# Row-by-row tiles at both ends of a four-layer graph network, with a layer's shifts made once and elu added a quarter at a time

## The chip, the cores and the metric

The kernel runs on one core of a Trainium2 chip, in one launch. The metric is the device time of the whole launch in microseconds (us), the median of several executions. One further execution was taken with the hardware profiler. Its instructions belong to TensorE (PE, whose weight loads are listed apart as PEld), VectorE (DVE), ScalarE (ACT), GpSimd (POOL) and SyncE (SP, which here only issues DMA transfers).

## What is computed

The input x holds 8 graphs (batches) of 2048 nodes with 128 features, and one 0/1 adjacency matrix of 2048 x 2048 serves all of them. Four layers follow one another; each adds to x a function of the normalized, rectified x. Layers 0 and 3 are graph attention with one head, layer 1 is attention with four heads under the same mask, layer 2 is a masked mean. What matters here are layers 0 and 3:

```python
e = leaky_relu(s1[:, :, None] + s2[:, None, :])          # slope 0.2
e = where(adj[None, :, :] > 0, e, very_negative)
h_prime = einsum('bij,bjo->bio', softmax(e, -1), h)      # layer 0: + h, then elu
```

s1 and s2 are two numbers per node, made from h. Each output row i needs a softmax over the 2048 nodes j, hence a maximum over the allowed j, the exponentials, their sum, and a product with h.

## The kernel before, in words

The 2048 nodes of a batch are 16 row tiles of 128. Four row tiles are a quarter (512 rows, one buffer of x). Layers 0 and 3 use six groups of row tiles, `GROUPS`: four of three tiles and two of two.

**A graph attention layer by groups** (`gat_loop`, L450) keeps the scores transposed: j is on the partitions and the rows i of a group lie along the free dimension, so the exponentials can go into TensorE as weights without a transpose. For this, two things must lie along the free dimension of every partition: s1 of the group's rows, and the shift m of each row (the leaky value of its maximum). The order of a group is:

- `gat_maximum` (L440 to L447): for each row tile, one DVE instruction of 128 x 2048 on a broadcast copy of s2 (`s2b`) and a mask (`pmg`, fetched from DRAM) gives the largest allowed s2 of each row, `mn`.
- `shifts` (L475 to L483): three DVE instructions of a few columns turn s1 and `mn` into `cab`.
- `spread` (L485), through `along_free` (L400 to L411): DVE transposes `cab` (L404), four transfers write the rows to DRAM (`rowd`, L407), and one reads them back to all 128 partitions (`ab`, L410).
- Eight steps `jp`, each for two j tiles: `leaky` (L510, two ACT instructions), `lowered` (L516, DVE), `exps` (L520, ACT), `masked` (L525, DVE), `product` (L536, 2 x 3 or 2 x 2 matmuls into `gacc`). The stages of successive steps overlap, each stage one step later than the one before it.
- `ended` and `closed` (L551 on): reciprocals, and the layer's own `finish`. In layer 0, `finish` makes `hq` on DVE (L663) and `ex` on ACT (L667), and adds elu to x with two DVE instructions for each row tile (L672, L673). In layer 3 it adds to x (L892), and when the row tile is the last of its quarter it stores the quarter.

`ahead(k)` prepares group k during the first five steps of group k - 1.

**The order of the work.** The order on PE, DVE, ACT and POOL is written out by hand; each engine works through its list in order. SP's order is set by a planner. There are three parts:

- The **head** (batch 0): the masks are made from the adjacency matrix, layer 0 of batch 0 runs by groups (with the maxima of a group inside the loop, and one empty step after each group), and a quarter goes on to the projections of layer 1 (`before_attention`) as soon as its row tiles are done.
- The **middle**: layer 1 of all batches, as `mains`, 256 blocks of 12 short steps. Between these steps stand the other layers of the neighbouring batches: layer 2, then layer 0 of the next batch, then layer 3 of the last one. `work` spreads a list of steps by weight; `locked` puts three steps of `mains` to each step of a `gat_loop`. In layer 0 of batches 1 to 7 all 16 maxima are made ahead, beside the aggregation of layer 2 (`merged(agg, top)`); in layer 3 they are made in the loop.
- The **tail**: layers 2 and 3 of batch 7, with nothing of layer 1 beside them.

Of the kernel before, what the change touches and what calls it, by code (L numbers as in the profile page):

```python
# [18 lines left out]
P = 128  # L19
# [12 lines left out]
def gnn_kernel(  # L32
# [201 lines left out]
    ones = const.tile([P, P], F32, name="ones")  # L234
# [5 lines left out]
    w0T = const.tile([P, P], F32, name="w0T")  # L240
# [159 lines left out]
    def along_free(col, dst, n):  # L400


        row = small("row", (P, 32))
        nc.vector.transpose(row, col)  # L404
        d = new(dr2, "rowd", "rowd", (T, P))
        for g in range(4):
            nc.sync.dma_start(  # L407
                out=d[0:n, g * 32 : (g + 1) * 32], in_=row[g * 32 : g * 32 + n, :]
            )
        nc.sync.dma_start(  # L410
            out=dst, in_=d[0:n, :].rearrange("t p -> (t p)").partition_broadcast(P)  # L411
        )
# [22 lines left out]
    def gat_rows(st):  # L435

        st["s2b"] = new(sp2, "s2b", "s2b", (P, N))
        along_free(st["s2n"], st["s2b"], T)
# [12 lines left out]
    def gat_loop(st, finish, maxima, gap):  # L451
# [23 lines left out]
        def shifts(k):  # L475
            i0, n = GROUPS[k]
            s1 = st["s1"][:, i0 : i0 + n]
            u = small("gu", (P, 3))[:, 0:n]
            nc.vector.tensor_tensor(u, s1, st["mn"][:, i0 : i0 + n], ALU.subtract)
            cab = next_of("cab", cabs)  # L480
            nc.vector.tensor_copy(cab[:, 0:n], s1)
            nc.vector.scalar_tensor_tensor(cab[:, n : 2 * n], u, ALPHA, u, ALU.mult, ALU.max)
            gr[k]["cab"] = cab  # L483

        def spread(k):  # L485
            n = GROUPS[k][1]
            t = new(abp, "ab", "ab", (P, 2 * n * P))
            along_free(gr[k]["cab"], t, 2 * n)
            gr[k]["s1"], gr[k]["m"] = t[:, 0 : n * P], t[:, n * P : 2 * n * P]

        def ahead(k):
            if k >= len(GROUPS):
                return []
# [65 lines left out]
        for fns in ahead(0):  # L559
            steps.add(2.0, *fns)  # L560

        items = []
        for k in range(len(GROUPS)):
            items += [(k, jp) for jp in range(T // 2)] + [None] * gap
# [3 lines left out]
        for step in range(len(items) + len(stages) - 1):  # L568
            fns = []
            if step < len(items) and items[step]:  # L570
                k, jp = items[step]
                if jp == 0:
                    nxt = ahead(k + 1)
                if 0 < jp <= len(nxt):
                    fns += nxt[jp - 1]
            for s in reversed(range(len(stages))):
                if 0 <= step - s < len(items) and items[step - s]:
                    fns.append(at(names[s], lambda f=stages[s], a=items[step - s]: f(*a)))
            steps.add(2.6, *fns)
# [75 lines left out]
    def layer0_loop(b, st, maxima=False, gap=1):  # L655
# [3 lines left out]
        def finish(i0, n, acc, rec):  # L659
            hq = new(hpp, "hp", "hp", (P, 3, P))  # L660
            ex = new(hpp, "ex", "ex", (P, 3, P))
# [7 lines left out]
            def add():  # L669
                for q in range(n):  # L670
                    xg = xb[(i0 + q) // 4][:, (i0 + q) % 4, :]
# [5 lines left out]
        return gat_loop(st, finish, maxima, gap)  # L677
# [174 lines left out]
    def layer3(b, gap=1, maxima=True):  # L852
# [35 lines left out]
        def finish(i0, n, acc, rec):  # L888
            for q in range(n):
# [5 lines left out]
                if it % 4 == 3:  # L895
                    g = it // 4
# [5 lines left out]

        tops = [at("maxi", lambda it=it: gat_maximum(st, it)) for it in range(T)]
        return pre, gat_loop(st, finish, maxima, gap), tops


# [354 lines left out]
    with tc.manual_schedule(engines=ENGINES):  # L1261
# [16 lines left out]
        loop = layer0_loop(0, st0, True)  # L1278
        quarters, queue, others = before_attention(0), [], masks_all[n:]
        start = len(loop) - 9 * len(GROUPS) - 6  # L1280
        for _ in range(3):
            run([others.pop(0)])
        n_late = len(others)
        for k, step in enumerate(loop):
# [3 lines left out]
            for g, group in enumerate((1, 2, 3, 5)):  # L1288
                if k == start + 9 * group + 13:
                    queue.extend(quarters([g]))  # L1290
            if queue:
                run([queue.pop(0)])
        run(others + queue)
# [76 lines left out]
        for b in range(B):  # L1370
            side = Steps()
            if b >= 1:
                pre2, agg = layer2(b - 1)
                side.extend(pre2)
                pre3, loop3, _ = layer3(b - 1, 0)
# [5 lines left out]
            if b + 1 < B:  # L1381
# [3 lines left out]
                side.extend(merged(agg, top) if agg else top)  # L1385
                loop0 = layer0_loop(b + 1, sts[b + 1], gap=0)

                side[-8:-8] = loop0[:5]
# [31 lines left out]
        pre3, loop3, _ = layer3(B - 1)  # L1420
# [60 lines left out]
```

## Time and profile before

| | |
|---|---|
| median of 3 runs | 4548.66 us (4547.90 to 4550.93) |
| the profiled execution | 4556.48 us, of which the span of its instructions is 4554.6 us |
| mean granted clock of TensorE | 0.956 of full speed |
| head: first matmul of layer 1 starts | 253.6 us |
| tail: layer 3's broadcast s2 (`s2b`) is used first | 4423.8 us |
| last store issued | 4551.3 us |

Times within the profile are microseconds from the span's start. A group row of the profile gives the line and engine, the operation, output and inputs by name, the shapes, how many there were, the busy time and the mean duration, and then the idle time of the engine just before them and what ended it. A matmul on 32-bit numbers has two records in the trace: the program has 4096 matmuls into `gacc`, the trace 8192. Where the text speaks of a pace, it is the distance from start to start; it is shorter than the duration, since an engine begins the next instruction before the last one is finished.

A table by stretches of time gives, for each stretch, its length, the busy time and number of instructions of each engine, the clock granted to TensorE as a share of full speed, the share of the DMA engines' time and their GB/s.

### The profile page before, as it was taken

The page shows a single profiled execution, that of the slowest core. Times are in us where ns is not written, and L with a number is a line of the kernel's source. Part 1 is how long each engine was busy: PE and PEld are TensorE (multiplying, and loading weights), DVE is VectorE, ACT ScalarE, POOL GpSimd, SP SyncE. Part 2 cuts the span into 40 slices and gives each one's busy share as a digit, 9 for nine tenths or more (in the row PEclk, how much of TensorE's full clock was granted, in tenths as well). Part 3 has the DMA queues.
Part 4 walks back from the last instruction along what each step waited for, and adds up shares of the span by engine and source line. Part 5 has one row for each costly group of instructions (what it writes and reads, how often), then busy time and mean ns, then how long its engine had stood idle before and what let it go on. Part 6 is the DMA issues. An engine that isn't in the chain of part 4 may idle for free.

```text
span 4554.6 us, 87375 instructions
## 1 busy us (share of the span) xinstructions
PE 4009.2 (88%) x33290; PEld 2809.7 (62%) x33290; DVE 3796.6 (83%) x7529; ACT 3613.6 (79%) x5121; POOL 553.7 (12%) x549
## 2 busy tenths in 40 slices
PE   3679998998999989998899988999899989998966
PEld 2545765666657666576666756566665766655636
DVE  5968877889889898888988889799888898748939
ACT  6658985898859888698868988598895989858916
POOL 1220011004100130002300031001300010000000
PEclk6889999999999999999999999999999999999978
DMA  8522133223241323313242232412333223222232
GB/s 305 153 69 59 54 92 110 66 71 106 82 140 53 94 83 107 109 60 105 77 128 75 67 101 84 144 49 72 102 103 116 59 69 113 58 75 71 64 100 75
DMA packets 312192, 423.32 MB, mean 93 GB/s; under 512 B 65318, under 2 KB 181724, under 8 KB 307676
## 3 DMA queue, kind: packets, MB, share of 16 engines
q1 hardware_dynamic: 311264, 417.51, 30.2%
q8 instruction: 263, 4.31, 0.4%
q14 instruction: 157, 1.29, 0.1%
q10 hardware_dynamic: 508, 0.22, 0.0%
HBM read 365.78 MB, written 55.98 MB: 93 GB/s over the span
## 4 chain that ended last, share of the span: by engine, by line
PE 31%; DVE 25%; ACT 22%; issue 5%; DMA 2%; SPq 0%; DVEq 0%; POOL 0%; ACTq 0%
PE pagg L798 7%; DVE e L963 7%; ACT e L970 6%; PE pt L982 6%; ACT eT L987 6%; PE gacc L536 6%; DVE dump L447 5%; PE sc L946 5%; ACT ge L510 5%; DVE ge L516 4%; DVE ge L525 3%; PE acc L997 3%; ACT ge L520 3%; DVE ln_s L341 1%; PE ph L397 1%
## 5 line engine op out<-in xcount | busy, mean ns | idle before, releaser
L987 ACT COPY eT<-pt 128x1024 f32<-128x1024 f32 x1024 | 996.2, 1017 | 440.8 <-PE pt L982 439.5
L536 PE MATMUL gacc<-haug,ge 128*128 128x129 f32 x8192 | 1106.6, 285 | 156.4 <-DVE ge L525 121.5
L982 PE MATMUL pt<-ident,e 128*128 128x128 f32 x8192 | 1043.7, 279 | 168.6 <-DVE amh L963 126.1
L536 PEld LDWEIGHTS gacc<-haug,ge 128*128 128x128 f32 x8192 | 1008.2, 197 | 297.7 <-issue 215.3
L982 PEld LDWEIGHTS pt<-ident,e 128*128 128x128 f32 x8192 | 928.2, 144 | 268.5 <-DVE amh L963 149.8
L970 ACT ACTIVATE e<-e,amn 128x2048 f32<-128x2048 f32 x512 | 1035.1, 2022 | 12.7 <-DVE amn L963 12.7
L510 ACT ACTIVATE ge<-ab,s 128x384 f32<-128x384 f32 (+1 forms) x1536 | 808.0, 583 | 107.7 <-DMA ab<-rowd 89.2
L963 DVE CUSTOM_DVE_ANT_0 e<-sc,pm 128x1024 f32<-128x1024 f32 x512 | 625.0, 1221 | 265.6 <-PE sc L946 220.6
L946 PE MATMUL sc<-ks,qr 32*128 32x512 f32 x4096 | 746.6, 658 | 59.5 <-ACT eT L987 41.5
L963 DVE CUSTOM_DVE_ANT_0 e<-sc,pm,amh 128x1024 f32<-128x1024 f32 x512 | 657.5, 1284 | 76.0 <-PE sc L946 3.6
L520 ACT ACTIVATE ge<-ge 128x768 f32<-128x768 f32 (+1 forms) x768 | 601.3, 784 | 134.0 <-DVE ge L516 133.1
L525 DVE SCALAR_TENSOR_TENSOR ge<-mg,ge 128x768 f32<-128x768 fp8e4 (+1 forms) x768 | 666.3, 868 | 24.4 <-ACT ge L520 23.9
L516 DVE TENSOR_TENSOR ge<-ge,ab 128x768 f32<-128x768 f32 (+1 forms) x768 | 665.7, 867 | 16.3 <-ACT ge L510 13.1
L447 DVE CUSTOM_DVE_ANT_0 dump<-s2b,pmg 128x2048 bf16<-128x2048 f32 x256 | 588.9, 2300 | 36.9 <-DMA pmg<-pm_all 18.3
L997 PE MATMUL acc<-eT,vv 128*32 128x256 f32 x8192 | 562.9, 393 | 1.9 <-ACT eT L987 1.9
L997 PEld LDWEIGHTS acc<-eT,vv 128*32 128x32 f32 x8192 | 216.3, 110 | 496.4 <-issue 407.7
L349 POOL TENSOR_SCALAR ln_r<-ln_mv 128x4 f32<-128x4 f32 x128 | 86.4, 675 | 3528.2 <-DVE ln_mv L343 3280.7
L946 PEld LDWEIGHTS sc<-ks,qr 32*128 32x128 f32 x4096 | 235.3, 187 | 222.4 <-ACT eT L987 112.6
L798 PE MATMUL pagg<-mt,hm 128*128 128x512 fp8e4 x1536 | 353.6, 380 | 11.7 <-DVE agT L816 11.7
L798 PEld LDWEIGHTS <-hm 128*128 128x128 bf16 x1536 | 148.0, 98 | 185.5 <-issue 31.4
L350 POOL TENSOR_TENSOR ln_r<-ln_r,neg_half 128x4 f32<-128x4 f32 x128 | 161.4, 1261 | 10.7
L383 PE MATMUL ptr<-ident,h 128*128 128x128 f32 x512 | 88.2, 297 | 41.1 <-DVE h L357 12.6
(131 smaller groups left out, 2591.3 us busy)
## 6 DMA issues: line engine op xcount, KB each, us to landing
pmg<-pm_all SPq DMA_DIRECT2D x256, 256.0 KB
mg<-mg_all SPq DMA_DIRECT2D x128, 384.0 KB
pm<-pm_all SPq DMA_DIRECT2D x128, 256.0 KB
qr<-qd SPq DMA_DIRECT2D x1024, 32.0 KB
mt<-mt_all SPq DMA_DIRECT2D x64, 512.0 KB
ab<-rowd SPq DMA_DIRECT2D x64, 384.0 KB
adj<-in_adj_dram SPq DMA_DIRECT2D x16, 1024.0 KB
s2b<-rowd SPq DMA_DIRECT2D x16, 1024.0 KB
```

Of the source, the lines that this page charges most:

```text
L447: nc.vector.tensor_tensor_reduce(dump, st["s2b"], pm, UP, HIGHEST, ALU.add, ALU.min, st["mn"][:, it : it + 1])
L510: nc.scalar.activation(e[:, c, :], gr[k]["s1"], AF.Prelu, bias=st["s2"][:, j : j + 1], alpha=ALPHA)
L516: nc.vector.tensor_tensor(e, e, bc_mid(gr[k]["m"], 2), ALU.subtract)
L525: nc.vector.scalar_tensor_tensor(e, mt, BIG, e, ALU.mult, ALU.min)
L536: nc.tensor.matmul(gr[k]["acc"][:, q, :], e[:, c, q * P : (q + 1) * P], st["haug"][:, j, :], start=(j == 0 and q == 0), stop=(j == T - 1), ...
L798: nc.tensor.matmul(st["pa"], st["hm"][:, j, s, :], st["mt", g, j // 8][:, j % 8, :], start=(j == 0 and s == 0), stop=(j == T - 1 and s == ...
L946: nc.tensor.matmul(blk["sc"][g // 2][:, (g % 2) * 512 : (g % 2 + 1) * 512], blk["q"][r, t * P : (t + 1) * P], ks_t[b, hh][r, :], start=Tru ...
L963: nc.vector.tensor_tensor_reduce(e[:, c], blk["sc"][h], pm[:, c], UP, least, ALU.add, ALU.min, to)
L970: nc.scalar.activation(blk["e"][t], blk["e"][t], AF.Exp, scale=-1.0, bias=blk["mn"][:, t : t + 1], accum_out=blk["ao"]["sum"][:, t, blk["h ...
L982: nc.tensor.transpose(pt[:, c, t, :], blk["e"][t][:, j * P : (j + 1) * P], ident)
L987: nc.scalar.copy(eT, blk.pop(("pt", w)).rearrange("p c t n -> p c (t n)"))
L997: nc.tensor.matmul(pair["acc"][g * HD : (g + 1) * HD, blk["hh"] % 2, :], vv_t[blk["b"], blk["hh"]][:, j, :], blk["eT"][w][:, g, :], start= ...
```

## The change

There are three parts.

**Row by row.** In the head's layer 0 and in the tail's layer 3 only the first three groups (row tiles 0 to 8) are worked by groups, and without the empty steps. The other seven row tiles (9 to 15) are worked row by row by the new `gat_rowwise`: i stays on the partitions and all 2048 j lie along the free dimension, so no `shifts`, no `spread` and no `gat_maximum` is needed; instead the exponentials must be transposed by TensorE and copied back. The two lists of steps are merged by weight, and the row-by-row list ends at 0.9 (head) or 0.85 (tail) of the other.

**Shifts once.** `along_free` is split into `to_rows` (transpose and four writes) and `from_rows` (the broadcast read). Where the maxima are made ahead, which is in layer 0 of batches 1 to 7, the shifts of all 16 row tiles are made once, with the first group, and each group reads its part with two transfers of half the size. Since these shifts need all 16 maxima, the maxima now end at 0.9 of the aggregation, and the first five steps of the loop are put three steps before the aggregation's end, where they stood eight before.

**elu by quarters.** `finish` of layer 0 adds elu with two DVE instructions for all row tiles of a group that lie in one quarter, where it had two for each row tile. A quarter goes on when its last row tile is done, in any order.

Two buffers of the start (`ones`, `w0T`) move into a rotating pool.

```diff
+    def to_rows(col, n):
         row = small("row", (P, 32))
         nc.vector.transpose(row, col)
-        d = new(dr2, "rowd", "rowd", (T, P))
+        d = new(dr2, "rowd" if n <= T else "rowa", "rowd", (T if n <= T else 2 * T, P))
         for g in range(4):
             nc.sync.dma_start(
                 out=d[0:n, g * 32 : (g + 1) * 32], in_=row[g * 32 : g * 32 + n, :]
             )
+        return d
+
+    def from_rows(d, i, n, dst):
         nc.sync.dma_start(
-            out=dst, in_=d[0:n, :].rearrange("t p -> (t p)").partition_broadcast(P)
+            out=dst, in_=d[i : i + n, :].rearrange("t p -> (t p)").partition_broadcast(P)
         )
...
+        def shifts(k):
+            i0, n = GROUPS[k]
+            if maxima:
+                gr[k]["cab"] = shifts_of(i0, n)
+            elif k == 0:
+                st["rowa"] = to_rows(shifts_of(0, T), 2 * T)
 
         def spread(k):
...
+            if maxima:
+                from_rows(to_rows(gr[k]["cab"], 2 * n), 0, 2 * n, t)
+            else:
+                for c in range(2):
+                    from_rows(st["rowa"], c * T + i0, n, t[:, c * n * P : (c + 1) * n * P])
...
+    def gat_rowwise(st, finish, its):
...
+        def leaky(it):
...
+            e[it] = new(ep, "e", "er", (P, N))
+            nc.scalar.activation(
+                e[it], st["s2b"], AF.Prelu, scale=ALPHA, bias=st["s1n"][:, it : it + 1],
+                alpha=1.0 / ALPHA,
+            )
+
+        def lowest(it):
+            pm = new(mg, "pm", "pmg", (P, N), I8)
+            nc.sync.dma_start(out=pm, in_=pm_all[it])
+            mn[it] = small("rmn", (P, 1))
+            nc.vector.tensor_tensor_reduce(
+                e[it], e[it], pm, UP, HIGHEST, ALU.add, ALU.min, mn[it]
+            )
+
+        def exps(it):
+            sm_[it] = small("rsum", (P, 1))
+            nc.scalar.activation(
+                e[it], e[it], AF.Exp, scale=-1.0, bias=mn.pop(it), accum_out=sm_[it]
+            )
+
+        def turned(it, h):
+            pt = psum("ptg", (P, 8, P))
+            for c in range(8):
+                j = 8 * h + c
+                nc.tensor.transpose(pt[:, c, :], e[it][:, j * P : (j + 1) * P], ident)
+
+            def read():
+                eT[it, h] = new(tp, "eT", "eTg", (P, 8, P))
+                nc.scalar.copy(eT[it, h], pt)
+
+            later(read)
+
+        def product(it, h):
+            if h == 0:
+                acc[it] = new(psa, "acc", "racc", (P, 1, P))
+            t = eT.pop((it, h))
+            for c in range(8):
+                j = 8 * h + c
+                nc.tensor.matmul(
+                    acc[it][:, 0, :], t[:, c, :], st["haug"][:, j, 0:P],
+                    start=(j == 0), stop=(j == T - 1),
+                )
+
+        def ended(it):
+            rec = small("rrec", (P, 1))
+            nc.vector.reciprocal(rec, sm_.pop(it))
+            close[it] = finish(it, 1, acc.pop(it), rec)
...
+        stages = [
+            (7, closed), (6, ended), (0, leaky), (1, lowest), (2, exps),
+            (3, lambda i: turned(i, 0)), (4, lambda i: turned(i, 1)),
+            (4, lambda i: product(i, 0)), (5, lambda i: product(i, 1)),
+        ]
...
             def add():
-                for q in range(n):
-                    xg = xb[(i0 + q) // 4][:, (i0 + q) % 4, :]
+                ended.update(range(i0, i0 + n))
+
+                for g in range(i0 // 4, (i0 + n - 1) // 4 + 1):
+                    lo, hi = max(i0, 4 * g), min(i0 + n, 4 * g + 4)
+                    xg = xb[g][:, lo - 4 * g : hi - 4 * g, :]
+                    q = slice(lo - i0, hi - i0)
                     nc.vector.scalar_tensor_tensor(xg, ex[:, q, :], 1.0, xg, ALU.min, ALU.add)
                     nc.vector.scalar_tensor_tensor(xg, hq[:, q, :], 0.0, xg, ALU.max, ALU.add)
...
-        loop = layer0_loop(0, st0, True)
+        loop = layer0_loop(0, st0, True, 0, [0, 1, 2], 0.9)
...
-                side.extend(merged(agg, top) if agg else top)
+                side.extend(merged(agg, top, 0.9) if agg else top)
                 loop0 = layer0_loop(b + 1, sts[b + 1], gap=0)
 
-                side[-8:-8] = loop0[:5]
+                n = len(side) - 3 * bool(agg)
+                side[n:n] = loop0[:5]
...
-        pre3, loop3, _ = layer3(B - 1)
+        pre3, loop3 = layer3(B - 1, 0, True, [0, 1, 2], 0.85)
```

In the numbers of the stages, a row tile starts every second step and its stage s runs s steps after its start.

## The prediction

> **What bounds the kernel now.** I read the page first, then the tables by stretches of time for the head, one layer 0 of the middle and the tail, then the groups and the order of time in the tail. The page says that nothing idles much on average, which hides that the stages differ:
>
> ```profile
> PE 4009.2 (88%) x33290; PEld 2809.7 (62%) x33290; DVE 3796.6 (83%) x7529; ACT 3613.6 (79%) x5121; POOL 553.7 (12%) x549
> ```
>
> The tables by stages tell them apart. Tail, then head, then a layer 0 of the middle:
>
> ```profile
> 4453.00:4463.00 10.00, 7.93 (x67) 7.43 (x66) 10.00 (x11) 7.29 (x14) 0.00 (x0) 1.00 0.45 129
> 4463.00:4473.00 10.00, 4.09 (x20) 4.12 (x21) 9.96 (x19) 5.54 (x10) 0.00 (x0) 0.66 0.25 70
> 4473.00:4483.00 10.00, 8.27 (x68) 7.69 (x68) 10.00 (x12) 7.71 (x14) 0.00 (x0) 1.00 0.26 84
> sum 132.00, PE 73.62 PEld 70.42 DVE 118.70 ACT 80.78 POOL 0.00; mean PE 5.66 PEld 5.42 DVE 9.13 ACT 6.21 POOL 0.00
> ```
> ```profile
> 130.00:155.00 25.00, 15.05 (x98) 14.10 (x96) 24.02 (x37) 15.01 (x25) 0.00 (x0) 0.80 0.80 191
> 180.00:205.00 25.00, 17.46 (x120) 15.12 (x119) 24.86 (x47) 17.56 (x31) 10.73 (x4) 0.93 0.42 122
> ```
> ```profile
> 1420.00:1440.00 20.00, 19.53 (x186) 14.47 (x181) 18.20 (x35) 20.00 (x31) 0.00 (x0) 1.00 0.12 32
> 1480.00:1500.00 20.00, 19.27 (x186) 14.10 (x185) 17.40 (x36) 20.00 (x33) 0.00 (x0) 1.00 0.22 77
> ```
>
> In both ends DVE is the bound (third engine column: full), with PE and ACT far below. In the middle's layer 0 ACT is full, PE nearly, and DVE has some 10% to spare. So DVE work is worth its time at the ends and little in the middle.
>
> **The ends, row by row.** First what a row tile costs by groups. In the tail's order of time L516 and L525 of three-tile groups start 0.87 us apart (4451.50, 4452.37, 4453.23), so a step jp takes 1.74 us of DVE; for two-tile groups 1.20 (a start each 0.60, head). Eight steps per group, plus a maximum (2.21 + 0.08):
>
> ```profile
> L510 ACT ACTIVATE ge<-ab,s 128x384 f32<-128x384 f32 x64 | 35.1, 601 | 23.2 <-DMA ab<-rowd 23.1
> L516 DVE TENSOR_TENSOR ge<-ge,ab 128x768 f32<-128x768 f32 x32 | 30.5, 953 | 5.7 <-ACT ge L510 5.7
> L525 DVE SCALAR_TENSOR_TENSOR ge<-mg,ge 128x768 f32<-128x768 fp8e4 x32 | 30.3, 947 | 0.0
> L447 DVE CUSTOM_DVE_ANT_0 dump<-s2b,pmg 128x2048 bf16<-128x2048 f32 x13 | 29.7, 2284 | 0.0
> L520 ACT ACTIVATE ge<-ge 128x768 f32<-128x768 f32 x32 | 26.9, 840 | 23.6 <-DVE ge L516 23.0
> ```
>
> (Groups of the tail; "x" is the count, then busy time and mean ns.) DVE of a loop before: 32 x 1.74 + 16 x 1.20 + 16 x 2.29 + 16 x 0.27 (L892) + small ones of 3 = 120; the trace has 118.7. After: 24 x 1.74 = 41.8, nine maxima 20.6, seven `lowest`, the closing 4.3 + 3. `lowest` is not in the trace; it is L447 with a 32-bit output. Below stands L447 (2.29), above the pair L963 of twice 1024 (1.22 + 1.28 = 2.50). I take 2.3, its nearest row: 16. **Sum 86, 34 less.**
>
> ACT before: 32 x 1.83 (starts of L520 in the tail: 4449.78, 4451.61) + 16 x 1.42 (two-tile) = 81; trace 80.8. After: 24 x 1.83 = 43.9 and, for each of seven rows, `leaky` of 2048 (L510 takes 493 ns for 256 and 601 for 384 elements, so 0.86 ns each, 2.03 us), `exps` (L970 of the same form, starts 1.98 apart) and two copies like L987 (0.92 apart): 5.85 x 7 = 41. **Sum 85, 4 more.** The slope could be off for `leaky`: between 1.6 (0.65 ns, the copy's 1024 in 0.92 doubled) and 2.2, so 3 less or 1 more.
>
> PE keeps its 256 products (two records each) and gains 112 transposes. Warm pace: 0.237 us for a product (12 weight loads of 6 products in 1.41), 0.216 for a transpose (L982, 16 loads of 8 in 1.73): 60.7 + 24.2 = 85. At the tail's present clock: 73.6 + 24.2/0.83 = 103. **PE becomes the bound, 85 to 103**, with DVE and ACT close behind.
>
> Here the clock decides. It was 1.00 from 4453 to 4463 and 0.66 from 4463 to 4473, where DVE did maxima and PE waited 6.5 us; in the middle, with PE over 90% busy, it is 1.00. Transposes fill these gaps, so I take 0.93: 91 us. The Trainium skill ("TensorE: Matmul & The Clock Gate", Part 1) says that a window of about 3.4 us without work halves the clock, which the row above agrees with; its Part 4 says that transpose-mode work does not count as busy, which speaks against this change. If that held, 112 transposes would leave the clock at today's, and the sum would be the 103 above. The middle, with L982 at its warm pace and 1.00, speaks for the other.
>
> Path in the tail. `s2b` is used at 4423.8. The first two masks are loaded; the third instruction on DVE is now row 9's `lowest`, whose mask needs the first buffer (free at 4426.1, landing 2.8 later as now), and the group's third maximum follows: `shifts` end near 4434.2 instead of 4431.7, `ab` lands near 4441 instead of 4438.6. In this time row 9 and 10 do `leaky`, `lowest` and `exps`, so PE starts near 4436 instead of 4447. Then 91 of PE, 4 for the time to 4441 when only a row's transposes are there, 4 for five last steps at ACT's 1.83 and the drain, and 4 which I choose for in-order engines that wait for each other with all three at 85: 4539 instead of 4551. **Tail 12 less** (bounds: 85 with nothing lost, 4525: 26 less; 103 and 10 lost, 4557: 6 more). At the very end one three-tile group closes two quarters, 0.3 of L892 and a second store (0.4 to issue): 0.7, inside these bounds.
>
> Head. DVE falls by the same 34, and by 1.3 for elu. But `shifts` of the first group come later: behind `lowest` of row 9 (2.3), its wait for a mask (about 3), and the degrees with 16 instructions L1234 (4.3, now ahead of it, as the masks' last steps fall into the first tenth of a shorter loop). `ab` lands near 120 instead of 109.4. From there PE has 256 x 0.25 + 112 x 0.22 + 9 for two quarters = 98, less 4 already done; the loop ends near 222 with 8 lost, instead of 242. Then two quarters (tiles 4 to 7 and 8 to 11 both wait for the last group) go on instead of one: 243.2 to 253.6 now, and 4 more for the second, whose instructions follow the first's on each engine, and 2.5 for a three-tile drain. 239 instead of 253.6. **Head 13 less** (bounds as in the tail: 24 less to 8 more).
>
> **The middle.** Per layer 0 of batches 1 to 7, shifts once take 5 x (0.16 x 3 + 0.20) = 3.4 us off DVE and 20 small writes off SP, and elu 32 x 0.29 = 9.2 becomes 16 instructions at 0.29, 0.42 or 0.56 (start overhead 0.16 and 0.133 per 128, from L672 and L829's 0.69 for 512) = 6.8. Together 5.8 us. It is beside ACT: in 1360 to 1540 ACT idles 3.3 of 180, so at most that much can come back; if ACT's cover were gone all 5.8 would count.
>
> Against it stands a wait that is moved. At the start of each layer 0 ACT waits for `ab`:
>
> ```profile
> 1344.29 0.21 DVE L404 STREAM_TRANSPOSE row<-cab 128x32 f32<-128x32 f32 x1
> 1353.47 1.12 ACT L510 ACTIVATE ge<-ab,s 128x384 f32<-128x384 f32 x2 [5.61 <-DMA ab<-rowd]
> ```
>
> The chain from the transpose through DRAM takes 9.2 us, of which 5.6 are waited, with layer 1's copies L987 and exponentials L970 queued behind. In the new order the same two copies and one exponential stand between transpose and `leaky`, and no maximum is left on DVE behind them. The first half of `ab` (192 KB) lands earlier than 384 KB did: the 4.9 us from issue to use may lose 1 or nothing; the wider writes (32 rows for 6) may add 1. Bounds: 2 less to 3.6 more (all 9.2 open). I take 0, and 1 us back from ACT's idle time: 7 x 1 = **7 less** (bounds 7 x 5 less, 7 x 3.6 = 25 more). Later groups read rows long written; `ab` waits there are few already.
>
> **Sum:** 12 + 13 + 7 = 32; the span 4554.6 becomes 4522.6, its execution 4524.5. That execution stood 7.8 above the median, so the median becomes 4548.7 - 32 = **4517**.
>
> **Rivals.**
> 1. *All three engines overlap well* and the clock is full: tail 20, head 20, middle 15: 4494. For it: each row stage has a step of slack. Against: in-order queues at equal load.
> 2. *They hold each other up*: PE waits for `exps`, ACT's copy for the transposes, DVE for `leaky`; a fifth of the time is lost: tail 4, head 5, middle 4: 4536.
> 3. *The middle gives the ends back*: `ab` at the start of seven layers is waited for with all 9.2 us: 25 more against 25 less: 4549. For it: the spread stands three steps ahead of the aggregation's end, not eight. Against: the order above.
> 4. *Slower: the clock stays low.* If PE stays near 0.66 in both ends, 85 becomes 129: tail ends 44 later than the 85 would, at 4436 + 129 + 12 = 4577 (26 more), head 20 more, middle 7 less: 4588. It decides where PE's work fills the present loop: 4551 - 4436 - 12 = 103, a mean clock of 85/103 = 0.83. For it: today's tail has just this mean. Against: the gaps that lower it are filled.
> 5. *It doesn't do what it says*: "once a layer" holds for seven layers only, since the middle's layer 3 makes its maxima in the loop; this is already in the sum.
>
> **Chances.** Forecast 45% (4502 to 4530), rival 1 17%, rival 2 20%, rival 3 9%, rival 4 9%. The measurement tells 0.2%, about 9 us, from no change. Faster: forecast, 1 and most of 2, 79%; same: part of 2 and 3, 10%; slower: 4 and part of 3, 11%. The range goes from rival 1 to just short of rival 3's time: 4492 to 4545.
>
> **What would show it.** In the tail: DVE busy near 86 and PE over 85 of the loop, clock above 0.9, 4539 or so for the last addition. PE under 80% busy beside a clock under 0.8 would show rival 4; all three engines near 80% busy, rival 2. `leaky` of a row at 2.0 us and `lowest` at 2.3. In the head: `ab` first used near 120, the first matmul of layer 1 near 239. In the middle: the wait for `ab` at the start of layer 0 still 5 to 6 us, ACT full after it. I am wrong if a wait for a mask (`pmg`, two buffers, now shared by maxima and rows) is large on DVE, or the middle's period of batches changes by over 3 us.

## The result, and the profile after

The changed kernel took **4542.0 us** (median of 10 runs, 4531.4 to 4545.3) beside 4550.6 for the kernel before on the same chip: a ratio of **0.9973** with a 95% interval of 0.9964 to 0.9982. That is 8.5 us faster, where 32 were forecast. The profiled execution took 4542.2 us with a span of 4540.4.

The span divides at the first and the last matmul `sc` of layer 1 into head, middle and tail:

| us | before | after | difference | forecast |
|---|---|---|---|---|
| head, to the first `sc` | 253.6 | 237.3 | -16.3 | -13 |
| middle | 4059.0 | 4084.1 | **+25.1** | -7 |
| tail, from the last `sc` | 242.0 | 218.9 | -23.1 | -12 |
| span | 4554.6 | 4540.4 | -14.2 | -32 |

(The profiled execution before lay 6 us above its median, the one after on it; so 14 in the spans are 8.5 in the medians.) Both ends gained more than forecast, and the middle lost most of it.

The page of the changed kernel, busy time of each engine:

```profile
PE 4028.9 (89%) x33514; PEld 2828.8 (62%) x33514; DVE 3703.9 (82%) x7159; ACT 3618.5 (80%) x5051; POOL 533.2 (12%) x549
```

DVE lost 93 us and ACT gained 5. As before, this average says nothing of where the time went. The table by stretches of the tail does (length, then PE, PEld, DVE, ACT, POOL with their counts, clock, DMA share, GB/s); the last line sums 4428 to 4540:

```profile
4448.00:4458.00 10.00, 5.13 (x23) 4.84 (x24) 6.25 (x6) 8.31 (x10) 0.00 (x0) 0.50 0.26 72
4458.00:4468.00 10.00, 8.75 (x64) 8.55 (x64) 8.38 (x14) 10.00 (x14) 0.00 (x0) 0.84 0.20 54
4468.00:4478.00 10.00, 8.91 (x80) 8.70 (x79) 8.62 (x11) 10.00 (x13) 0.00 (x0) 1.00 0.35 105
4488.00:4498.00 10.00, 9.05 (x66) 8.93 (x67) 9.85 (x19) 6.82 (x11) 0.00 (x0) 0.83 0.26 82
4508.00:4518.00 10.00, 9.57 (x86) 9.37 (x85) 6.90 (x9) 10.00 (x17) 0.00 (x0) 1.00 0.01 2
sum 112.00, PE 78.75 PEld 76.51 DVE 86.21 ACT 82.63 POOL 0.00; mean PE 7.16 PEld 6.96 DVE 7.84 ACT 7.51 POOL 0.00
```

DVE, which was full in such stretches before, now has 1.4 to 3.1 of 10 us to spare in three of these, where ACT is full and PE close behind; from 4488 to 4498 DVE still leads (9.85) and ACT has 6.82. Over the whole 112 us no engine works more than 86. The head and a layer 0 of the middle, in the same columns:

```profile
130.00:155.00 25.00, 21.69 (x164) 20.92 (x164) 22.61 (x32) 25.00 (x34) 0.00 (x0) 0.87 0.77 205
180.00:205.00 25.00, 22.14 (x192) 21.57 (x193) 19.11 (x33) 23.95 (x36) 0.00 (x0) 1.00 0.18 57
1420.00:1440.00 20.00, 19.53 (x184) 14.08 (x179) 17.93 (x32) 20.00 (x30) 0.00 (x0) 1.00 0.24 51
1480.00:1500.00 20.00, 19.28 (x187) 14.10 (x185) 17.13 (x33) 20.00 (x32) 0.00 (x0) 1.00 0.26 90
```

Well inside a layer 0 the middle looks as before: ACT full, and DVE 0.3 us lower in each stretch of 20. So the 25 us are not lost there. I counted layer 1's blocks (one exponential of 128 x 2048 each, 64 in a batch) and took the time from block 8 to block 24 of each batch; the start of the next layer 0 lies in it. For batches 1 to 6 (the starts near 1357, 1893, 2433 and so on) these six stretches together take **886.0 us before and 909.7 after, 23.7 more**. With the same stretch of batch 0 (81.2 and 85.1) it is 27.6, and the rest of the middle took 2.5 less. There the wait of DVE's `y` (the end of layer 2) for its input `hb` stands out; before, then after (total us, times, longest):

```profile
DVE y L829 <- DMA hb<-hb_all: 14.5, 6, 3.2
```
```profile
DVE y L939 <- DMA hb<-hb_all: 55.4, 7, 10.1
```

The order of time at one start after the change (start, us, engine or queue, line, operation, tile, count, and in brackets the idle time before it and what ended it):

```profile
1342.09 0.21 DVE L404 STREAM_TRANSPOSE row<-cab 128x32 f32<-128x32 f32 x1
1342.33 1.70 SPq L407 DMA_DIRECT2D rowd<-row  x4
...
1347.54 1.76 SPq L414 DMA_DIRECT2D ab<-rowd  x4
1349.35 0.43 SPq L468 DMA_DIRECT2D mg<-mg_all  x1
1349.82 0.43 SPq L935 DMA_DIRECT2D hb<-hb_all  x1
1351.19 1.12 ACT L523 ACTIVATE ge<-ab,s 128x384 f32<-128x384 f32 x2 [5.87 <-DMA ab<-rowd]
...
1356.82 0.69 DVE L939 TENSOR_TENSOR y<-pn,hb 128x512 f32<-128x512 f32 x1 [10.09 <-DMA hb<-hb_all]
...
1357.56 2.08 PE L1060 MATMUL sc<-ks,qr 32*128 32x512 f32 x4 [3.18 <-DVE y L939]
```

The same place before:

```profile
1344.52 1.40 SPq L407 DMA_DIRECT2D rowd<-row  x4
...
1348.48 0.32 SPq L410 DMA_DIRECT2D ab<-rowd  x1
1349.04 0.32 SPq L445 DMA_DIRECT2D pmg<-pm_all  x1
1349.40 0.43 SPq L825 DMA_DIRECT2D hb<-hb_all  x1
1349.88 0.43 SPq L464 DMA_DIRECT2D mg<-mg_all  x1
...
1354.87 0.69 DVE L829 TENSOR_TENSOR y<-pn,hb 128x512 f32<-128x512 f32 x1 [2.35 <-DMA hb<-hb_all]
```

Before, one `ab` (384 KB) and a mask `pmg` (256 KB) went just ahead of `hb`, and `hb` was issued 5.1 us after the row's transpose and used 5.5 later. Now four `ab` transfers (two for the first group and, since the row already holds every group's shifts, two for the second) and a mask `mg` (768 and 384 KB) go ahead of it: issued 7.7 us after the transpose, used 7.0 later. From the transpose to `y` it is 14.7 us instead of 10.6. PE then waits 3.2 us for `y`.

### The profile page after: what moved, and what is told of

It reads as the page before. It is cut to its first block, busy times and chain, and to the rows that moved or that the text cites. A ratio compares the mean times of both kernels' runs of the same rounds, so it can differ in the third digit from the quotient of the medians.

```text
span 4540.4 us, 87141 instructions
## 1 busy us (share of the span) xinstructions
PE 4028.9 (89%) x33514; PEld 2828.8 (62%) x33514; DVE 3703.9 (82%) x7159; ACT 3618.5 (80%) x5051; POOL 533.2 (12%) x549
## 4 chain that ended last, share of the span: by engine, by line
PE 35%; DVE 24%; ACT 20%; issue 4%; DMA 2%; SPq 1%; DVEq 0%; POOL 0%; ACTq 0%
PE pt L1096 7%; PE pagg L908 7%; DVE e L1077 7%; PE gacc L549 7%; PE sc L1060 5%; ACT e L1084 5%; ACT eT L1101 5%; DVE dump L451 4%; ACT ge L523 4%; DVE ge L529 4%; PE acc L1111 3%; DVE ge L538 3%; ACT ge L533 2%; DVE ln_s L341 1%; DMA hb<-hb_all 1%
## 5 line engine op out<-in xcount | busy, mean ns | idle before, releaser
L549 PE MATMUL gacc<-haug,ge 128*128 128x129 f32 x7744 | 1024.7, 281 | 42.3 <-DVE x L1002 17.0
L549 PEld LDWEIGHTS gacc<-haug,ge 128*128 128x128 f32 x7744 | 934.0, 194 | 173.3 <-issue 122.1
L523 ACT ACTIVATE ge<-ab,s 128x384 f32<-128x384 f32 (+1 forms) x1440 | 765.3, 591 | 90.1 <-DMA ab<-rowd 76.6
L538 DVE SCALAR_TENSOR_TENSOR ge<-mg,ge 128x768 f32<-128x768 fp8e4 (+1 forms) x720 | 628.3, 873 | 37.1 <-ACT ge L533 36.8
L533 ACT ACTIVATE ge<-ge 128x768 f32<-128x768 f32 (+1 forms) x720 | 571.1, 795 | 100.8 <-DVE ge L529 100.7
L529 DVE TENSOR_TENSOR ge<-ge,ab 128x768 f32<-128x768 f32 (+1 forms) x720 | 626.6, 870 | 17.2 <-ACT ge L523 13.0
L451 DVE CUSTOM_DVE_ANT_0 dump<-s2b,pmg 128x2048 bf16<-128x2048 f32 x242 | 557.2, 2302 | 45.8 <-DMA s2b<-rowd 20.0
L349 POOL TENSOR_SCALAR ln_r<-ln_mv 128x4 f32<-128x4 f32 x128 | 80.7, 630 | 3562.6 <-DVE ln_mv L343 3448.1
```

What stands on the lines that cost most here:

```text
L451: nc.vector.tensor_tensor_reduce(dump, st["s2b"], pm, UP, HIGHEST, ALU.add, ALU.min, st["mn"][:, it : it + 1])
L523: nc.scalar.activation(e[:, c, :], gr[k]["s1"], AF.Prelu, bias=st["s2"][:, j : j + 1], alpha=ALPHA)
L529: nc.vector.tensor_tensor(e, e, bc_mid(gr[k]["m"], 2), ALU.subtract)
L538: nc.vector.scalar_tensor_tensor(e, mt, BIG, e, ALU.mult, ALU.min)
L549: nc.tensor.matmul(gr[k]["acc"][:, q, :], e[:, c, q * P : (q + 1) * P], st["haug"][:, j, :], start=(j == 0 and q == 0), stop=(j == T - 1), ...
```

## The experiments

My theory A was: the middle loses its time because `hb` stands on SP's queue behind the moved and prefetched transfers. Rival B: the moved chain of `ab` itself costs it. Rival C: the time is lost elsewhere, with the waits only its sign.

All kernels, with the ratio to the kernel before as measured beside it; the stretches are blocks 8 to 24, of batch 0 and of batches 1 to 6 together. Head and tail are those of the table above.

| kernel | us | ratio, 95% interval | head | tail | batch 0 | 1 to 6 |
|---|---|---|---|---|---|---|
| before | 4550.6 | 1 | 253.6 | 242.0 | 81.2 | 886.0 |
| the change | 4542.0 | 0.9973 (0.9964 to 0.9982) | 237.3 | 218.9 | 85.1 | 909.7 |
| hb_ahead | 4510.1 | 0.9910 (0.9897 to 0.9924) | 236.1 | 213.8 | 85.5 | 886.4 |
| shifts_by_group | 4504.9 | 0.9899 (0.9886 to 0.9913) | 237.2 | 215.1 | 81.5 | 882.5 |
| ends_by_groups | 4565.3 | 1.0031 (1.0021 to 1.0042) | 247.6 | 241.4 | 85.0 | 903.8 |
| ends_alone | 4514.5 | 0.9916 (0.9903 to 0.9930) | 236.4 | 214.7 | 81.4 | 884.7 |
| by_group_hb_ahead | 4496.3 | 0.9876 (0.9859 to 0.9893) | 237.2 | 212.9 | 81.5 | 872.1 |
| rows_4 | 4535.5 | 0.9959 (0.9944 to 0.9973) | 246.9 | 228.2 | 81.2 | 885.4 |
| rows_10 | 4510.5 | 0.9906 (0.9889 to 0.9924) | 237.2 | 213.4 | 81.2 | 886.3 |
| hb_ahead_batch1 | 4504.5 | 0.9897 (0.9877 to 0.9918) | 235.4 | 213.8 | 81.6 | 885.2 |
| maxima_early | 4498.1 | 0.9869 (0.9855 to 0.9884) | 236.3 | 212.4 | 80.7 | 871.8 |
| elu_by_tile | 4506.4 | 0.9886 (0.9869 to 0.9902) | 238.7 | 213.3 | 81.5 | 873.3 |
| degrees_late | 4494.8 | 0.9860 (0.9846 to 0.9875) | 234.2 | 212.6 | 81.8 | 874.9 |
| shifts_earlier | 4555.2 | 1.0001 (0.9993 to 1.0010) | 237.4 | 212.4 | 85.7 | 930.8 |
| by_group_late_place | 4502.7 | 0.9889 (0.9872 to 0.9906) | 239.1 | 214.3 | 85.0 | 872.6 |

One warning on small differences: shifts_by_group, rows_4 and rows_10 have the same code in the middle, and their middles took 4049.5, 4057.9 and 4058.9 us. What a single profile shows of the whole middle below some 9 us is therefore no finding; the stretches of blocks 8 to 24 repeat better (882.5, 885.4 and 886.3). The head is the same code in eight versions (the change, hb_ahead, shifts_by_group, by_group_hb_ahead, hb_ahead_batch1, maxima_early, shifts_earlier, by_group_late_place) and ended between 235.4 and 239.1.

**hb_ahead**: the change, with `hb` fetched earlier.

```diff
+        def load_hb(g):
+            st["hb", g] = chunk("hb")
+            nc.sync.dma_start(out=st["hb", g], in_=flat(hb_all[g]))
...
-            hb = chunk("hb")
-            nc.sync.dma_start(out=hb, in_=flat(hb_all[g]))
+            hb = st.pop(("hb", g))
...
+                if q == 4:
+                    fns.append(lambda g=g: load_hb(g))
```

> The changed kernel, but layer 2's bias block `hb` of a quarter is fetched in the fifth step of that quarter's aggregation instead of just before its use, so that on SP it stands ahead of the first group's `ab` and mask. Theory A (the 25 us lost in the middle are the wait of DVE's `y` for `hb`, 8.0 to 10.1 us at six starts of layer 0 where it was 1.9 to 2.5, because `hb` is issued behind four `ab` halves and a mask): the wait for `hb` falls under 1 us, the middle (from layer 1's first matmul to its last) returns to 4059 from 4084, the time to about 4515, 25 to 35 less than the changed kernel. Rival B (the start is late because ACT waits for `ab`, 4 to 6 us, whatever `hb` does): DVE then waits for ACT instead, at most 10 less. Rival C (the denser maxima beside the aggregation cost it): nothing changes, 4542.

It took 4510.1: 29 us less than the change by the ratios. The same start of layer 0:

```profile
1339.76 1.76 SPq L414 DMA_DIRECT2D ab<-rowd  x4
1341.32 0.69 DVE L942 TENSOR_TENSOR y<-pn,hb 128x512 f32<-128x512 f32 x1 [1.92 <-PE pn L937]
1341.57 0.43 SPq L468 DMA_DIRECT2D mg<-mg_all  x1
...
1343.50 1.12 ACT L523 ACTIVATE ge<-ab,s 128x384 f32<-128x384 f32 x2 [5.51 <-DMA ab<-rowd]
```

`y` now waits for PE alone and runs 6.6 us after the row's transpose (1334.77). The four `ab` are as they were, and ACT still waits 5.5 us for them, so what came back was not theirs. Theory A holds as far as `hb` goes: the stretches take 23.3 us less, and the middle is at 4063.0, where 4059 was expected. The tail is 5.1 shorter too, 4.6 of it before layer 3's `s2b` is used: layer 2's last quarter had waited 3.2 us for its `hb` there. That the 23.3 are about the 23.7 that the change had added does not make `hb` the whole cause, since the kernel before lost time to `hb` as well; by_group_hb_ahead and by_group_late_place take the two apart.

**shifts_by_group**: the second part of the change undone, the others left.

```diff
-            if maxima:
-                gr[k]["cab"] = shifts_of(i0, n)
-            elif k == 0:
-                st["rowa"] = to_rows(shifts_of(0, T), 2 * T)
+            gr[k]["cab"] = shifts_of(i0, n)
...
-                side.extend(merged(agg, top, 0.9) if agg else top)
+                side.extend(merged(agg, top) if agg else top)
...
-                n = len(side) - 3 * bool(agg)
-                side[n:n] = loop0[:5]
+                side[-8:-8] = loop0[:5]
```

> The changed kernel with its second part undone: in layer 0 of batches 1 to 7 the shifts are made for each group again, the loop's first steps stand eight steps ahead of the aggregation's end and the maxima are not drawn together. Ends by rows and elu by quarters stay. Theory A and rival B: the waits at the start of layer 0 are those of the kernel before (`ab` 5.4, `hb` 2.3), the middle is 4059 or a little less, the time about 4510 (head 16 and tail 23 less than before stay). Rival C expects the same of this one. If instead the loss comes from elu by quarters or from a head that hands over differently, the middle stays near 4084 and the time near 4542.

4504.9, 34 us less than the change by the ratios. Making the shifts once, with the places that go with it, costs more than all that the change gains net.

**ends_by_groups**: both ends by six groups again (`layer0_loop(0, st0, True)` and `layer3(B - 1)`).

> The changed kernel with its first part undone: all six groups at both ends, with the empty steps. Shifts once and elu by quarters stay. Theory A, B and C: the middle still loses 25, the ends gain nothing but 1 to 2 from elu in the head: about 4572, slower than before by 0.5%. If the loss in the middle were a consequence of the earlier hand-over at the head, it would be near 4550.

4565.3: slower than the kernel before, and the stretches still lose 17.8 us, so the loss in the middle does not come from the earlier hand-over at the head. Without the rows the tail is back at 241.4; the head keeps 6 of its 16 us. What is left there of the change is elu, the quarters that go on as soon as they are done, and the two moved buffers; which of them brings the 6 us was not tried. So the rows bring 10 us in the head and 22.5 in the tail.

**ends_alone**: rows at both ends, shifts by group, elu by row tile.

> The first part alone: ends row by row; shifts by group and elu by row tile as before. All theories: head 15 and tail 23 less, middle as before: about 4513. Against the kernel with shifts by group it prices elu by quarters in the middle's seven layers, where I expect 0 to 7 us more here (DVE has slack beside ACT).

4514.5, as expected: the ends by themselves are worth 0.84%.

**by_group_hb_ahead**: shifts_by_group and hb_ahead together.

> Shifts by group (the version that took 4504.9) with `hb` fetched in step 4 of its quarter, ahead of the loop's DMAs. Theory A (what the six layer starts lose is the place of `hb` in SP's queue): the 8.8 us in 4 waits of DVE for `hb` that were left in the middle go to 0, and 3 to 8 us of the time with them: 4497 to 4502. Rival B (those four waits stand beside a full ACT and cost nothing): 4505. Were the earlier fetch itself harmful (it takes a buffer and the queue from the aggregation's masks), over 4508.

4496.3, just under what theory A said: no wait of `y` for `hb` is left (of the four one, 3.3 us, was in the tail), and the stretches fall from 882.5 to 872.1. The kernel before had such waits too (14.5 us), so a fault that the change made worse was there before it. Fetching `hb` ahead is worth 10.4 us in the stretches with the shifts by group and 23.3 with the shifts made once. With `hb` out of the way in both, shifts once still cost 886.4 - 872.1 = 14.3 us.

**rows_4** and **rows_10**, on shifts_by_group: the groups `[0, 1, 2, 3]` with 4 rows, and `[0, 1]` with 10, in both ends.

> Shifts by group, and four groups and only 4 rows in both ends (in the change three groups and 7 rows). Per row tile, work by rows takes 4.9 us off DVE and adds 2.1 us of transposes to PE (112 in 17.1 us in the tail after the change, so 0.15 each). In the tail's loop DVE goes from 86 to 101 us and PE from 79 to 72. Theory D (DVE still bounds the ends): 10 to 15 us more at each end, 4525 to 4535 against 4504.9. Theory P (PE bounds the ends, as the prediction said): 6 less at each end, 4493. Theory E (no engine bounds them; the waits between the three do): within 5 of 4505.

> Shifts by group, and two groups and 10 rows in both ends. In the tail's loop DVE goes from 86 to 72 us, PE from 79 to 85, ACT from 83 to 85. Theory D (DVE bounds the ends): 10 less at each end, 4485. Theory P (PE bounds them): 6 more at each end, 4517. Theory E (the waits between the three): within 5 of 4505, or more if rows alone at the end of the loop have no group steps beside them.

With 4 rows head and tail take 9.7 and 13.1 us longer than with 7 (3.0 of the 13.1 before `s2b` is used, so outside the loop): theory D up to there. With 10 rows the head is the same and the tail 1.7 shorter: DVE is the bound no longer, and no other engine is enough of one to cost 5 us. The table by stretches, each the 102 us from the first use of `s2b`, for 4, 7 (shifts_by_group) and 10 rows (with 4 rows the loop goes on for some 12 us more):

```profile
4415.00:4517.00 102.00, 62.63 (x492) 60.26 (x492) 89.18 (x123) 73.43 (x105) 0.00 (x0) 0.81 0.27 79
```
```profile
4394.00:4496.00 102.00, 77.52 (x621) 75.80 (x622) 85.16 (x115) 82.73 (x107) 0.00 (x0) 0.85 0.22 65
```
```profile
4403.00:4505.00 102.00, 80.53 (x672) 78.07 (x672) 72.02 (x99) 85.59 (x98) 0.00 (x0) 0.92 0.20 54
```

The lead goes from DVE (89) to a tie (85 and 83) to ACT (86), and PE leads in none of them. (The time of rows_10 is 5.6 us above that of 7 rows, 3 by the ratios, although both its ends are no longer; that lies in the middle, in the spread named above.)

**hb_ahead_batch1**: hb_ahead, with batch 1's layer 0 (it stands in batch 0's stretch) by groups and its five steps eight before the end.

> `hb` fetched ahead (4510.1 as it was), and for batch 1 alone the shifts by group and the loop's first five steps eight before the end of the maxima, as before the change. Theory A' (the 5 us that are still lost against shifts by group come from batch 1's layer 0, where 16 maxima stand in one row before the loop): the first 64 blocks of layer 1 take 422 us instead of 425.9, and the time falls by 4 to 4506. Rival (they come from all batches alike, from the maxima that end at 0.9 of the aggregation): the first 64 blocks fall, the time stays at 4509 to 4511 since the later ones give it back, or both stay.

4504.5; its ratio can't be told from that of hb_ahead, but the stretches can: batch 0's falls from 85.5 to 81.6, the others stay, as theory A' said. The first 64 blocks took 424.1 us, where 422 was expected. The later by_group_late_place has the shifts by group and the late place, and 85.0; so these 4 us belong to the place of the five steps, not to the shifts.

**maxima_early**: by_group_hb_ahead with `merged(agg, top, 0.9)`, that is, the maxima of a layer 0 packed into 0.9 of the aggregation.

> Shifts by group and `hb` ahead (4496.3 as it was), and only the maxima of a layer 0 end at 0.9 of the aggregation, as the change has them. Theory M (with `hb` ahead, what shifts once still costs is that the denser maxima hold DVE up late in the aggregation: 1 to 2.4 us in blocks 8 to 16 of each batch): about 10 more, 4506, lost in blocks 8 to 16. Rival N (it is lost at the loop's start, by the wait for the shifts of all 16 row tiles): within 3 of 4496.

4498.1 and stretches of 871.8: theory M fell. Denser maxima cost nothing here.

**elu_by_tile**: by_group_hb_ahead with elu as before the change (`for q in range(n)`).

> Shifts by group and `hb` ahead (4496.3 as it was), and elu is added by row tile as before the change. As predicted, elu by quarters takes 2.4 us off DVE in each layer 0, hidden beside a full ACT in the middle, and 1.3 in the head, where DVE counts: 1 to 4 more, 4497 to 4500. Rival Q (2.4 us count in all eight layers 0): 17 to 20 more, 4514. The pair run with `hb` not ahead differed by 9.6 us.

4506.4, between the two theories. In one layer 0 the two instructions' rows went from 9.1 us to 6.6 with quarters, just what was forecast; by the ratios that is worth 5 us here and 8 between ends_alone and shifts_by_group, and both pairs of intervals overlap. So rival Q is out, but 1 to 4 us can't be told from 5 to 8.

**degrees_late**: by_group_hb_ahead, with the degrees behind the first group's shifts in the head.

```diff
-            if others and (k + 1) * n_late >= 0.1 * len(loop) * (n_late - len(others)):
+            if others and k >= (12 if len(others) == 1 else 0) and (
+                (k + 1) * n_late >= 0.1 * len(loop) * (n_late - len(others))
+            ):
```

> Shifts by group and `hb` ahead (4496.3 as it was), and the degrees with their 16 DVE instructions of 4.3 us stand behind the first group's shifts in the head. Theory L (the head ends when it does because `ab` lands at 126.8 and not at 120): the head ends 3 to 6 us earlier, first matmul of layer 1 at 232 to 234 instead of 237.2, time 4491 to 4493. Theory D (DVE bounds the head, and the 4.3 us have only been moved): 237, 4496.

`ab` is used first at 119.7 instead of 126.1, and the head ends 3.0 us earlier, at 234.2. That lies between the two theories and only just outside the spread of equal heads (235.4 to 239.1). In the time it can't be told from by_group_hb_ahead. At 0.9860 (0.9846 to 0.9875) this is the lowest ratio of all, 62 us under its before of 4556.7.

**shifts_earlier**: hb_ahead with the maxima ending at 0.7 of the aggregation and the five steps eight before its end.

> The change with `hb` fetched ahead (4510.1 as it was), the maxima of layer 0 ending at 0.7 of the aggregation and the loop's first five steps eight steps before the aggregation's end again, so that the shifts of all 16 row tiles are made once and still early. Theory W (what shifts once costs beside `hb`, 14 us against shifts by group with `hb` ahead, is the wait for `ab` at the start of a layer 0 that has moved to three steps before the aggregation's end): 10 to 14 less, 4496 to 4500, blocks 8 to 24 of batches 1 to 6 in 145.5 us as by groups (146 to 151 now). Rival V (it is the write of 32 rows and the two reads for each group, wherever they stand): 4508 to 4511.

4555.2: 41 us more by the ratios, the opposite of theory W. Eight steps before had meant something else in the old order, where maxima stood among these eight; now they were eight steps of the aggregation alone, most of a quarter. Of one stretch of 10 us:

```profile
1350.00:1360.00 10.00, 9.44 (x63) 4.89 (x60) 3.22 (x5) 1.12 (x2) 0.00 (x0) 1.00 0.82 234
```

PE aggregates, and ACT (1.1 of 10 us) and DVE (3.2) have nothing: ACT waits 5.8 us for `ab` and then 5.3 for PE. The six stretches took 930.8 us instead of 886.4. Of the 44.4, 37.5 stand in block 15. The run does not tell whether the shifts themselves or their place cost the rest; the next one does.

**by_group_late_place**: everything as in hb_ahead, places too, but the shifts by group.

> Shifts by group and `hb` ahead (4496.3 as it was), with the maxima ending at 0.9 of the aggregation and the loop's first five steps three steps before its end, both as the change has them. Theory W2 (the place costs the 14 us that are left): 4507 to 4512, with blocks 8 to 24 of batches 1 to 6 in 146 to 151 us. Theory V (the shifts made once cost them: one chain for 16 row tiles, wider writes, two reads): 4495 to 4499, blocks 8 to 24 in 145.5.

The time, 4502.7, lies between the two theories; the stretches decide. They take 872.6, as in by_group_hb_ahead: theory V. So with the places equal, the kernel that makes the shifts once takes 886.4 - 872.6 = 13.8 us more over six starts. The blocks, each from the start of its exponential to that of the next, show where (sums over batches 1 to 6):

| us | blocks 8 to 14 | 15 | 16 | 17 to 23 |
|---|---|---|---|---|
| before | 443.8 | 61.4 | 48.4 | 332.4 |
| the change | 453.4 | 58.2 | 66.5 | 331.5 |
| hb_ahead | 453.4 | 59.1 | 39.3 | 334.5 |
| by_group_hb_ahead | 443.7 | 59.0 | 39.3 | 330.0 |
| by_group_late_place | 453.4 | 49.9 | 39.3 | 330.0 |

In block 15 ACT waits for `ab`, in block 16 `y` for `hb`. Shifts made once cost 9.2 us in block 15. The 4.5 in blocks 17 to 23 stand in two batches alone, so they are not counted to the shifts: blocks 18 to 23 take 47.2 us in every batch of hb_ahead and by_group_late_place, at a granted clock of 1.00, except in batches 4 and 5 of hb_ahead, where they take 48.8 and 50.2 at 0.96 and 0.93. The late place costs 9.6 us in blocks 8 to 14, and by group it gives 9.1 back in block 15. Block 16 is 18.1 us longer in the change than before, and 9.1 shorter than before where `hb` is fetched ahead.

The start in batch 5, first by group, then once (hb_ahead):

```profile
2933.51 0.21 DVE L404 STREAM_TRANSPOSE row<-cab 128x32 f32<-128x32 f32 x1
2933.75 1.27 SPq L407 DMA_DIRECT2D rowd<-row  x4
...
2936.01 0.34 SPq L414 DMA_DIRECT2D ab<-rowd  x1
...
2939.98 1.13 ACT L516 ACTIVATE ge<-ab,s 128x384 f32<-128x384 f32 x2 [3.21 <-DMA ab<-rowd]
```
```profile
2937.72 0.21 DVE L404 STREAM_TRANSPOSE row<-cab 128x32 f32<-128x32 f32 x1
2937.95 1.70 SPq L407 DMA_DIRECT2D rowd<-row  x4
...
2940.83 1.76 SPq L414 DMA_DIRECT2D ab<-rowd  x4
...
2946.45 1.12 ACT L523 ACTIVATE ge<-ab,s 128x384 f32<-128x384 f32 x2 [5.51 <-DMA ab<-rowd]
```

From the transpose to ACT's first use it takes 6.5 us by group and 8.7 once. Over the six starts ACT's wait is 2.7 to 3.6 us by group and 4.2 to 5.5 once: the wider write takes longer to issue, the reads are issued 0.6 us later and are four instead of one. Which of these makes the wait longer was not tried.

## Why the prediction was wrong

That 4542 lies within the stated range, near its end, is luck, since two errors partly cancel: the ends gained 39.4 us in the profiled executions where 25 were forecast, and the middle lost 25.1 where 7 were to be gained.

**The ends: right in kind, too small.** DVE's tail sum was forecast at 86 and is 86.2; ACT's at 85 and is 82.6; a row's `lowest` takes 2.29 us (2.3) and `leaky` 1.99 (2.03):

```profile
L621 DVE CUSTOM_DVE_ANT_0 er<-er,pmg 128x2048 f32<-128x2048 f32 x7 | 16.0, 2286 | 0.5 <-DMA pmg<-pm_all 0.5
L612 ACT ACTIVATE er<-s2b,s1n 128x2048 f32<-128x2048 f32 x7 | 13.9, 1994 | 10.8 <-DVE s1n L609 10.8
L649 PE MATMUL racc<-haug,eTg 128*128 128x128 f32 x224 | 32.3, 305 | 12.3 <-ACT eTg L639 5.7 <-DVE x L1002 5.4 <-DVE row L404 1.2
L635 PE MATMUL ptg<-ident,er 128*128 128x128 f32 x112 | 17.1, 306 | 19.7 <-ACT er L627 19.7
```

(Groups of the tail after the change. In the prediction the terms of DVE's loop before add up to 119 and not to 120, and 493 and 601 ns for 256 and 384 elements are 0.84 ns each and not 0.86; neither matters here.) In order of time, from 4468 to 4478, where the clock was 1.00:

```profile
4469.68 1.04 PE L635 MATMUL ptg<-ident,er 128*128 128x128 f32 x8
4470.56 1.95 PE L649 MATMUL racc<-haug,eTg 128*128 128x128 f32 x16
```

The term that was mis-sized is "0.216 for a transpose (L982, 16 loads of 8 in 1.73)". The last two groups show the slip: 112 products have 224 records, but 112 transposes have 112, so that two records for a matmul holds for products alone. So the 16 loads at L982 were 16 transposes at 0.108 us, not 8. With that, PE's sum is 60.7 + 12.1 = 72.8, or 78 at the clock of 0.93 that I took, where I had 91; measured are 78.75. (That this comes so near is in part luck: the sum counts paces, the measurement durations that overlap.) The tail would have been forecast 25 less, and is 23 less. "PE becomes the bound" was therefore wrong, and rows_4 and rows_10 show what holds in its place: DVE with 4 rows, and with 7 and 10 none alone. Head and tail came out near rival 1's 20 and 20.

The head's sum has the same slip of 12 us: without it 25 less would have been forecast, and it is 16. The wait for a mask that I put at row 9's `lowest`, "about 3", is nothing there; the third maximum waits 8.1 for its own:

```profile
106.80 2.29 DVE L451 CUSTOM_DVE_ANT_0 dump<-s2b,pmg 128x2048 bf16<-128x2048 f32 x1 [8.07 <-DMA pmg<-pm_all]
```

With it `ab` is first used at 126.8, not 120. By degrees_late 6.4 us of such delay are worth about 3 at the head's end, little more than the spread. The other 6 us of the head were not traced.

**The clock: near what was taken.** From 4458 to 4528 it was 1.00 in five of the seven stretches of 10 us and 0.83 or 0.84 in two, and 1.00 from 155 to 205 in the head, with transposes among the products in all of them. Over the whole 112 us it was 0.84, because it stood at 0.50 until 4458, where PE worked 8.8 of 30 us; weighted by PE's busy time in the eleven stretches it was 0.91, where I took 0.93. Rival 4, with 0.66, did not happen. The Trainium skill's page "TensorE: Matmul & The Clock Gate", Part 4, says that transpose-mode work does not count as busy in the way that products do. The sum of 103 that I drew from that holds the wrong price of a transpose; with 0.108 us it is 73.6 + 12.1/0.83 = 88, and 78.75 was measured. Whether transposes count can't be told from these rows: later products stand between them, and early in the loop neither 16 transposes alone (3.68 us from 4442.4) nor 8 products alone (3.78 us from 4451.8) had lifted the clock from 0.50 by 4458.

**The middle: the step that failed.** It is "I take 0, and 1 us back from ACT's idle time: 7 x 1 = 7 less". I priced the wait for `ab` and found it about unchanged, which it is: 4.0 to 5.9 us at the starts after, 4.1 to 5.6 before. What I put at nothing, by leaving it out, is the wait behind the queue that the transfers moved into. The first group's `ab` and the second group's, which nothing holds back any longer, were issued on SP ahead of `hb`; and the maxima that had covered DVE's wait for `hb` had been moved away (no run separates these two). In block 16, where `y` waits, the six starts lost 18.1 of their 23.7 us. hb_ahead took 29 us back by moving that one transfer, but that is more than the change had added there: in the kernel with shifts by group the same move is worth 10.4 in the stretches. The rest, 6.4 us net in blocks 8 to 15, is the late place, which costs 9.6, and a wait for `ab` that gave only 3.2 of it back. The form of rival 3 (the middle gives the ends back) came true, for the greater part by another wait than its own.

Other faults of the step: my reason for 0, that the first half of `ab` lands earlier, did not hold. The late place alone shortens the wait to about 3.3 us, but the shifts made once lengthen it by some 1.6 (by_group_late_place), which cancels to the nothing that I had forecast, while the place itself costs what its shorter wait saves. And batch 0's layer start, which I did not look at, lost 4 us by the place. elu was priced rightly in DVE time (2.5 us in a layer 0, forecast 2.4); what it is worth in time, 5 or 8 us by intervals that overlap, is not settled.

**What I said would show it wrong**: the wait for masks on DVE did not in sum (9.9 us in all, 18.3 before), though 8.1 of it is the one wait in the head. The period of batches did: batches 0 to 3 of layer 1 took 6.0, 5.6, 5.4 and 3.1 us longer than before (4 to 6: 0.1 less, 0.8 and 2.3 longer).

## What to carry over

When transfers are moved forward or become ready sooner, list what the same queue issues right behind them, and who waits for it: 18 of the 24 us lost at six layer starts went to one late transfer of 256 KB that the change does not touch. A wait that is small today may be small only because work that you are about to move stands ahead of it. When a repair gives back about what a change has lost, apply it to the kernel without the change too: here 10 of the 23 us would have come back there as well. And before a price is taken from a record, count records against the program's operations for that very operation: here products have two and transposes one.

## What was not expected of the hardware

- A transfer issued behind more on the same queue landed later also after its own issue: `hb`, 256 KB, was used 7.0 us after its issue behind four `ab` and a mask (1152 KB), and 5.5 us behind one `ab` and a mask (640 KB). No run changed this alone. The Trainium skill ("DMA: Bandwidth & Descriptors", section "Queues, rings and completion order") says that descriptors of one queue are consumed in ring order on each DMA engine, which these rows agree with.
- A transpose of 128 x 128 32-bit numbers by TensorE takes half of what a product of that size does: 8 in 1.04 us beside 16 records, that is 8 products, in 1.95 (tail, at a clock of 1.00).
- Kernels with identical code in the middle differ there by 9 us of 4050 in their profiled executions (4049.5 to 4058.9). The clock granted over the shortest was 0.98 and over the two others 0.97; what sets that was not tried.
